# Windowed attention scores on Trainium2: penalty matmuls moved from the end to the front of a PSUM bank

## The chip, the cores and the metric

The kernel runs on one core of one Trainium2 chip. The metric is the device time of one execution in microseconds; the kernel before took 3160.31 us (median of three runs, 3152.64 to 3162.91).

## The reference, cut to what matters

Four layers are applied to an input of shape (4, 256, 48, 48), each as `x = x + layer(group_norm(x))`: an attention over 49 dilated taps, a convolution with binary weights, one with ternary weights, and layer 3, a linear attention over windows. Only layer 3 is touched:

```python
q = sigmoid(einsum('bchw,oc->bohw', x, Wq)); k = sigmoid(einsum('bchw,oc->bohw', x, Wk))
v = einsum('bchw,oc->bohw', x, Wv); v = v / max(norm(v, axis=channel_of_head), 1e-12)
for w in (1, 2, 4):                      # windows of 48, 24 and 12 rows and columns
    ws = H // w
    wk, wkv = box_sum(k, ws), box_sum(outer(k, v), ws)
    attn = einsum('bdhw,bdfhw->bfhw', q, wkv) / (einsum('bdhw,bdhw->bhw', q, wk) + 1e-6)
    outs.append(attn)
o = concatenate(outs, axis=1)
out = einsum('bchw,oc->bohw', o, Wout) + bout
```

There are 8 heads of 32 channels. A query at (row, column) sees the keys within half a window of it in both directions: 24, 12 or 6 rows and columns. Sigmoids are positive, so every score q.k is positive.

## The kernel before, in words

Layers 0 to 2 fill the time up to about 1416 us of the profiled execution, with the first projections of layer 3 among them. From there layer 3 computes numerators as masked scores times values.

**Tiling.** A block is one batch (4), one half of the channels with four heads (2) and one band of 8 rows (6): 48 blocks, in that order. Keys come in tiles of 8 rows by 16 columns, which makes 128 keys on the partitions, three tiles (`c` = 0, 1, 2) in a band. Queries are the moving operand, ordered by column and then by row: one column of the image is 8 elements.

**Steps.** `steps_of(rb)` (L1984) cuts a block into steps. A step holds the scores of four heads in two PSUM tiles `s` of two banks each, one bank of 512 fp32 for each head; the first tile is the pair of heads 0 and 1, the second that of heads 2 and 3. The pool `ps_s` has just these two tiles, so each step writes the banks that the step before it left. There are these kinds, counted over one batch and channel half (six bands):

- 32 *near* steps (`add_half`, L1968), for key bands within one band of the queries. A half has two products, each with its key tile: 320 columns of the moving operand for one and 192 for the other, which fill the bank.
- 12 *far* steps (`add_far`, L1954), for key bands three away: 280 and 168 columns, or 320 and 192.
- 8 *packed* steps with strips (`add_strips`, L1946) for key bands two away: three products of 128 columns for the widest window's strips, and one of 117 or 112 columns for the middle window.
- 6 packed steps that hold only products of the middle window (156 and 108, 84 and 81, or all four).

**Penalties.** The widest window is seen wholly by part of each tile; these keys are summed beforehand and added as a window state (`whole`, L2136). The rest, called the *strip*, needs a mask. The mask is added in PSUM: a bf16 matmul of `picks` (24 rows: 8 key rows and 16 key columns) with a row of costs adds -1024 where a key is not seen, and a ReLU in the evacuation makes these scores zero. `penalties()` (L165) lists the costs: for near steps the strip of each half (192 columns), for packed steps all four strips (384 columns), for far steps the whole tile (448 or 512). `PENALTY_AT` holds where each begins in the constant tile `masks`, which is loaded once, in bf16 (L1629).

**The order on TensorE.** `scores` (L2028) issues first the products, in the order product, pair, head, and then the penalties for each pair and head. The first product has `start=True`, the last penalty closes the bank. Four heads use four groups of 32 rows of the array. In the trace each fp32 product leaves two weight loads and two matmuls per head, a bf16 penalty one of each.

**Around it.** The loop over `stream` at the end of layer 3 issues for each step `n`: its scores, their evacuation (`masked`, L2055), and then the value products `acc` of step `n - 2` (`sums`, L2161). The evacuation is VectorE's mask multiplication for the middle window (`middle`) and a ReLU for the widest window (`widest`, on ScalarE, in far steps also on VectorE); the mask for the smallest window runs on GpSimd from SBUF. `acc` uses 128 rows by 32 columns of the array, `s` 32 rows by 128 columns. After each step `advance` lets background jobs (projections, key sums, norms, output products) issue a piece, within a budget that comes from `mask_time` and `sums_time`; these read `lo`, `hi` and `parts` of a step, not its products. Every engine runs its instructions in the order of the program (`InOrder`, L257), so the operations of a helper all carry L265 in the profile.

Of the kernel before, what the change touches and what calls it, by code (L numbers as in the profile page):

```python
# [23 lines left out]
B, C, H, W = 4, 256, 48, 48  # L24
# [3 lines left out]
RB = 8  # L28
# [66 lines left out]
def cols_seen(wi, c):  # L95
    h = HALVES[wi]
    return max(0, c * KC - h + (wi > 0)), min(W, c * KC + KC + h)


def cols_whole(c):  # L100

    return max(0, c * KC + KC - HALVES[0]), min(W, c * KC + HALVES[0])


def whole_ranges():
# [13 lines left out]
MID = W // 2  # L119
PARTS = [  # L120
    [(0, *cols_seen(0, 0)), (1, 0, MID)],
    [(1, MID, W), (2, *cols_seen(0, 2))],
]


def parts_seen(wi, half):

    got = []
    for c, x0, x1 in PARTS[half]:
        p0, p1 = cols_seen(wi, c)  # L130
        got.append((c, max(x0, p0), min(x1, p1)))
    return got


def strips(half):

    got = []
    for c, x0, x1 in PARTS[half]:
        f0, f1 = cols_whole(c)
        got.append((c, x0, f0) if x0 < f0 else (c, f1, x1))  # L140
    return got


def strip_columns(half):

    (_, x0, x1), (_, y0, _) = PARTS[half]
    (_, p0, p1), (_, q0, q1) = strips(half)
    assert p1 == x1 and q0 == y0
    return (p0 - x0) * RB, (x1 - x0 + q1 - q0) * RB
# [6 lines left out]
STRIPS = {}  # L156
# [7 lines left out]

def penalties():  # L165

    got = []
    for half in range(2):
        got.append(((0, half), strips(half), None))
    every = [(c, *part) for c, parts in STRIPS.items() for part in parts]  # L170
    got.append(((0, "strips"), every, None))
    for da, rows in FAR_ROWS.items():
        for half in range(2):
            got.append(((da, half), PARTS[half], rows))
    return got


def penalty_size(parts, rows):
    r0, r1 = rows or (0, RB)
    return sum(x1 - x0 for _, x0, x1 in parts) * (r1 - r0)  # L180


PENALTY_AT, _at = {}, 0
for _key, _parts, _rows in penalties():
    PENALTY_AT[_key] = _at, penalty_size(_parts, _rows)
    _at += PENALTY_AT[_key][1]
NPENALTY = _at
MASK_AT = [0, 0, MROWS[1] * MCOLS[1]]
PICK_AT = MASK_AT[2] + MROWS[2] * MCOLS[2]
PEN_AT = PICK_AT + P  # L190
NMASK = PEN_AT + NPENALTY
SM_ROOM = max(
# [5 lines left out]
def window_masks():  # L198
# [5 lines left out]
    for h, nr, m0, ncol in list(zip(HALVES, MROWS, MCOL0, MCOLS))[1:]:  # L204
# [4 lines left out]
        ms.append((rows[:, None, :] & cols[:, :, None]).reshape(P, -1))  # L209
    picks, costs = np.zeros((D, P)), np.zeros((D, NPENALTY))  # L210
    picks[ki, np.arange(P)] = 1
# [57 lines left out]
def conv_preact_kernel(  # L269
# [344 lines left out]
    with (  # L614
# [159 lines left out]
        def prepare_layer2():  # L774
# [34 lines left out]

            sums = smx.tile([P, NCT, 2, 2], F32, tag="sums", name="sums", bufs=1)  # L810
            pool.memset(sums, 0.0)
            yield
            ps = ps_cv.tile([P, 512], F32, tag="cv3", name="sum_ps")[:, 0 : 2 * NCT]
# [280 lines left out]
        def load_row(pool_, tag, a):  # L1094

            t = pool_.tile([P, NCT, K0, P], F32, tag=tag, name="wrow")
            sync.dma_start(
                out=t, in_=w1[:, a * K0 : (a + 1) * K0, :].rearrange("(ct p) k o -> p ct k o", p=P)
            )
            return t  # L1100
# [442 lines left out]
        with tc.tile_pool(name="wst", bufs=1) as wst:  # L1543
            for ct in range(NCT):
                fetch_x(0, ct)
            rows = [load_row(k1p, "k1", 0), load_row(vp, "v", MT), load_row(vp, "v", MT - 1)]
# [43 lines left out]
        with (  # L1590
# [11 lines left out]
            first = ExitStack()  # L1602
# [18 lines left out]
            for b in range(B):  # L1621
                if b + 1 < B:
                    filler = conv0(b + 1, {})
                else:
# [3 lines left out]
                    masks = wts3.tile([P, NMASK], BF16, name="masks")  # L1628
# [15 lines left out]
    with (  # L1644
# [14 lines left out]
        mask = {  # L1659
            i: masks[:, MASK_AT[i] : MASK_AT[i] + MROWS[i] * MCOLS[i]].rearrange(  # L1660
                "p (c r) -> p c r", c=MCOLS[i]
# [9 lines left out]
        for h in range(HEADS):  # L1671
            g = h % HG * D
# [245 lines left out]
        def rows_seen(wi, a, rb):  # L1918

            h = HALVES[wi]  # L1920
            return (
                max(0, a * RB - h + 1 - rb * RB),
                min(RB, a * RB + RB + h - rb * RB),
            )
# [5 lines left out]
        class Step:  # L1930
# [15 lines left out]
            def add_strips(self, a):  # L1946
                begin = self.columns
                for c, ranges in STRIPS.items():
                    at = self.add(a, c, ranges, (0, RB))
                    self.parts[0].append((a, c, ranges, (0, RB), at, self.columns - at))  # L1950
                self.penalties.append((begin, self.columns, PENALTY_AT[0, "strips"][0]))
                self.lo, self.hi = begin, self.columns

            def add_far(self, a, half):  # L1954
# [13 lines left out]
            def add_half(self, a, half):  # L1968

                da = a - self.rb  # L1970
                left = {}
                for c, x0, x1 in PARTS[half]:
                    left[c] = self.add(a, c, [(x0, x1)], (0, RB)) - x0 * RB
                self.lo, self.hi = strip_columns(half)
                self.penalties.append((self.lo, self.hi, PENALTY_AT[0, half][0]))
                for c, p0, p1 in strips(half):
                    self.parts[0].append((a, c, [(p0, p1)], (0, RB), left[c] + p0 * RB, (p1 - p0) * RB))
                for wi in range(1, NW):
                    rows = rows_seen(wi, a, self.rb)
                    for c, p0, p1 in parts_seen(wi, half):  # L1980
                        n = (p1 - p0) * (rows[1] - rows[0])
                        self.parts[wi].append((a, c, [(p0, p1)], rows, left[c] + p0 * RB, n))
# [35 lines left out]
        class Block:  # L2018
# [8 lines left out]

            def scores(self, st):  # L2028
                ss = [ps_s.tile([P, 2, 512], F32, tag="s", name="s") for _ in range(NPR)]
                for a, c, ranges, (r0, r1), at, n in st.products:  # L2030
                    for pr, s in enumerate(ss):
                        for j in range(2):
                            head = slice((2 * pr + j) * D, (2 * pr + j + 1) * D)
                            pe.matmul(
                                s[:, j, at : at + n],
                                kvs[self.b, self.ct, a][0][head, c, :],
                                of_columns(self.qs[head], ranges, r0, r1),
                                start=(at == 0),
                                stop=not st.penalties and at + n == st.columns,
                            )  # L2040
                for lo, hi, first in st.penalties:
                    for pr, s in enumerate(ss):
                        for j in range(2):
                            g = 2 * pr + j
                            rows = slice(g * D, g * D + RB + KC)
                            pe.matmul(
                                s[:, j, lo:hi],
                                picks[rows, :],
                                masks[rows, PEN_AT + first : PEN_AT + first + hi - lo],
                                start=False,  # L2050
                                stop=True,
                            )
                return ss

            def masked(self, st, ss):  # L2055

# [104 lines left out]
            def sums(self, wi, st, sms):  # L2161

                todo, acc = self.todo[wi], self.accs[wi]
                rows_ = acc.rearrange("p (w r) -> p w r", w=W)
                for k, (a, c, ranges, (r0, r1), _, _) in enumerate(st.parts[wi]):
                    for ranges_, o, n in self.alike(wi, ranges, r1 - r0):
                        for j in range(HG):
                            pe.matmul(
                                of_columns(rows_[D * j : D * (j + 1)], ranges_, r0, r1),
                                kvs[self.b, self.ct, a][1][:, c, j, :],  # L2170
                                sms[wi, k][:, j, o : o + n],
                                start=not self.reached[wi],
                                stop=(st is todo[-1] and k == len(st.parts[wi]) - 1),
                            )
                        for x0, x1 in ranges_:
                            self.reached[wi].update(range(x0, x1))
                if st is todo[-1]:
                    if self.i in inverses:
                        dve.tensor_mul(self.stage[:, wi, :], acc, inverses[self.i][:, wi, :])
                        divided.add((self.i, wi))  # L2180
                    else:
                        act.copy(self.stage[:, wi, :], acc)

        def of_columns(t, ranges, r0, r1):

# [110 lines left out]
        left = [groups[g] for g in made_first.left]  # L2296
# [88 lines left out]
        for n in range(len(stream) + LAG):  # L2385
            if n < len(stream):
                i, st, at, last = stream[n]
                if at == 0:
                    begun(i)
                ss = blocks[i].scores(st)  # L2390
# [3 lines left out]
            if n >= LAG:  # L2394
                i, st, at, last = stream[n - LAG]
# [64 lines left out]
```

## Time and profile before

| | us |
|---|---|
| median of three runs | 3160.31 |
| profiled execution | 3175.78 |
| its span, first to last instruction | 3174.0 |
| TensorE matmuls busy | 2852.3 |
| from 1416 us on: span / TensorE / GpSimd / VectorE / ScalarE busy | 1758 / 1661.2 / 1192.1 / 1074.4 / 712.3 |
| score products `s<-qs,ks`, 8704 records | 593.5 |
| penalties `s<-masks`, 1664 records | 169.2 |
| value products `acc<-sm,vs`, 18432 records | 606.6 |

PE stands for TensorE's matmuls, PEld for its weight loads, DVE for VectorE, ACT for ScalarE, POOL for GpSimd, SP for SyncE. A row of the groups names the tiles written and read, the shape and the count, then the busy time and the mean of one in ns, then the idle time of the engine before them and what ended it. In a shape such as 32*128 the first number is the rows and the second the columns of the array that are in use. Matmuls overlap, so the mean of one is longer than the distance from start to start; where a duration of streaming is wanted, the distance of starts is used. "issue" is time in which an engine waited for nothing that the profile shows.

### The profile page before, as it was taken

To read this page: it belongs to the slowest core of one execution; us is meant where nothing else is said; L and a number is where in the kernel's file an instruction comes from. 1 tells how busy PE (TensorE), PEld (TensorE's weight loads), DVE (VectorE), ACT (ScalarE), POOL (GpSimd) and SP (SyncE) were. 2 spreads that over 40 slices of the span, in tenths; PEclk is the share of its full clock that TensorE was granted. 3 is DMA by queue.
4 is the path that set the end of the run, shared out by engine and by line. 5 is a ranking of instruction groups with operands and counts; after the bars stand their busy time and mean duration, and the time that the engine had idled before them with its cause. 6 is when DMAs were issued, how large, how long until landed. Compare 5 with 4: busy or idle time off the path is not lost.

```text
span 3174.0 us, 99454 instructions
## 1 busy us (share of the span) xinstructions
PE 2852.3 (90%) x43082; PEld 2034.6 (64%) x43082; DVE 1989.3 (63%) x3779; ACT 991.4 (31%) x1959; POOL 1368.6 (43%) x1963
## 2 busy tenths in 40 slices
PE   3678999899989987889998899998999999999999
PEld 2556868677767866576665456665656666567665
DVE  7976658747864842276777565776546775555454
ACT  0002211121011134326643235552336533333322
POOL 0000012002000313046788876787856787744443
PEclk9889799999999998889999899999999999999999
DMA  8756412441333145324555665655644455611322
GB/s 277 214 161 188 154 68 103 127 127 49 132 114 113 57 124 158 113 80 138 160 181 174 184 203 157 183 174 161 169 127 145 142 173 156 166 41 43 97 73 66
DMA packets 380040, 434.10 MB, mean 137 GB/s; under 512 B 129843, under 2 KB 335443, under 8 KB 378451
## 3 DMA queue, kind: packets, MB, share of 16 engines
q1 hardware_dynamic: 378403, 425.76, 43.4%
q8 instruction: 341, 5.59, 0.7%
q0 software_dynamic: 144, 1.17, 0.2%
q10 hardware_dynamic: 1056, 0.79, 0.1%
q14 instruction: 96, 0.79, 0.1%
HBM read 288.11 MB, written 140.68 MB: 135 GB/s over the span
## 4 chain that ended last, share of the span: by engine, by line
PE 63%; DVE 11%; ACT 3%; POOL 3%; DMA 3%; issue 3%; SPq 1%; ACTq 0%; DVEq 0%; POOLq 0%
PE s L265 17%; PE cv L265 15%; PE acc L265 15%; PE out_ps L265 6%; PE proj_ps L265 5%; PE ap L265 3%; DVE sm L265 2%; DVE l2v L265 2%; ACT sm L265 1%; DVE v L265 1%; POOL sm L265 1%; PE keys_ps L265 1%; SPq L265 1%; DVE x L265 1%; DVE k L265 1%
## 5 line engine op out<-in xcount | busy, mean ns | idle before, releaser
L265 DVE TENSOR_TENSOR sm<-s,masks 128x448 f32<-128x448 f32 (+9 forms) x1408 | 620.1, 496 | 451.2 <-PE s L265 392.4
L265 POOL TENSOR_TENSOR sm<-sm,masks 128x704 f32<-128x704 f32 (+11 forms) x512 | 596.5, 1186 | 495.8 <-DVE sm L265 495.2
L265 ACT ACTIVATE sm<-s 128x384 f32<-128x384 f32 (+2 forms) x736 | 440.8, 608 | 734.2 <-PE s L265 583.9
L265 PE MATMUL cv<-vx,wt 128*128 128x288 f32 x2080 | 566.7, 429 | 90.5 <-DVE vx L265 49.2
L265 PE MATMUL s<-qs,ks 32*128 32x320 f32 (+10 forms) x8704 | 593.5, 361 | 36.7 <-ACT sm L265 26.3
L265 PE MATMUL acc<-sm,vs 128*32 128x128 f32 (+19 forms) x18432 | 606.6, 276 | 2.5 <-issue 2.1
L265 PEld LDWEIGHTS s<-qs,ks 32*128 32x128 f32 x8704 | 397.8, 186 | 264.1 <-issue 124.3
L265 PEld LDWEIGHTS acc<-sm,vs 128*32 128x32 f32 x18432 | 443.1, 110 | 176.5 <-issue 124.5
L265 PEld LDWEIGHTS cv<-vx,wt 128*128 128x128 f32 x2080 | 406.9, 200 | 213.6 <-issue 53.3
L265 POOL MEMSET v<- 128x16 f32 (+1 forms) x120 | 18.6, 214 | 765.2 <-DVE vx L265 639.0
L265 PE MATMUL cv<-v,wl 128*128 128x384 f32 x1152 | 227.2, 358 | 25.8 <-DVE x L265 8.2
L265 PEld LDWEIGHTS cv<-v,wl 128*128 128x128 f32 x1152 | 217.1, 198 | 37.0 <-issue 16.9
L265 DVE TENSOR_SCALAR sm<-s 128x896 f32<-128x896 f32 (+1 forms) x96 | 110.8, 1154 | 112.0 <-PE s L265 93.6
L265 PE MATMUL s<-masks 24*128 24x192 bf16 (+3 forms) x1664 | 169.2, 284 | 0.8 <-issue 0.8
L265 POOL TENSOR_TENSOR v<-l2v,v 128x384 fp32r<-128x384 f32 x96 | 108.4, 1158 | 119.5 <-ACT v L265 110.7
L265 PE MATMUL cv<-pad,wl 128*128 128x384 bf16 x864 | 145.6, 331 | 5.1 <-ACT pad L265 5.1
L265 POOL TENSOR_TENSOR nhi<-nhi,nq 128x384 f32<-128x384 f32 x144 | 147.3, 1044 | 0.0
L265 PE MATMUL out_ps<-o,wout_sb 128*32 128x384 f32 x1152 | 121.3, 490 | 7.2 <-ACT ns L265 3.7
L265 PEld LDWEIGHTS <-wl 128*128 128x128 bf16 x864 | 84.5, 98 | 65.6 <-issue 8.1
L265 PE MATMUL out_ps<-stage,wout_sb 128*32 128x384 f32 x1152 | 121.3, 487 | 0.0
L265 PE MATMUL ap<-seen,xT 120*128 120x120 f32 (+3 forms) x832 | 120.8, 306 | 0.0
L265 DVE TENSOR_TENSOR pt<-cs 128x184 f32<-128x184 f32 x144 | 120.4, 840 | 0.1
(176 smaller groups left out, 3398.6 us busy)
## 6 DMA issues: line engine op xcount, KB each, us to landing
wt<-wt SPq DMA_DIRECT2D x48, 768.0 KB
kb_d<-pt SPq DMA_DIRECT2D x48, 576.0 KB
rc<-r_d SPq DMA_DIRECT2D x192, 144.0 KB
nhi<-kb_d SPq DMA_DIRECT2D x120, 192.0 KB
nlo<-kb_d SPq DMA_DIRECT2D x88, 192.0 KB
o_d<-stage SPq DMA_DIRECT2D x24, 576.0 KB
o<-o_d SPq DMA_DIRECT2D x24, 576.0 KB
wl<-wl_d SPq DMA_DIRECT2D x16, 768.0 KB
```

What stands on the lines that cost most here:

```text
L265: return lambda *args, **kwargs: self.tc.keep_in_program_order(op(*args, **kwargs))
```

## The change

- The costs of near steps are no longer the strips alone. `whole_parts(half)` takes the strip of one tile and the whole columns of the other, which lie side by side in the bank: 320 columns for each half. The two halves form one table of 640 columns. The strips' table of the packed steps is dropped: `of_penalties` reads the four strips as two runs of 192 columns out of the near table. `NPENALTY` goes from 2688 to 2560.
- `scores` issues the penalties first. They carry `start=True`; products then have `start=False` wherever a step has penalties, and the last product closes the bank. Steps without penalties keep their order.
- No product may lie across the edge of the penalties, so `add_half` cuts at the strip: the 320 columns become 192 and 128. A near step has three products (192, 128, 192) in place of two.
- `lo`, `hi`, `parts` and so the evacuation, the value products and the budgets of the background jobs stay.

```diff
+def whole_parts(half):
+    first, second = PARTS[half]
+    return [strips(half)[0], second] if half == 0 else [first, strips(half)[1]]
...
 def penalties():
-    got = []
-    for half in range(2):
-        got.append(((0, half), strips(half), None))
-    every = [(c, *part) for c, parts in STRIPS.items() for part in parts]
-    got.append(((0, "strips"), every, None))
+    (c0, x0, _), (c1, y0, y1) = whole_parts(0)
+    (d1, z0, z1), (d2, _, w1) = whole_parts(1)
+    assert c1 == d1 and y1 == z0 == MID
+    got = [((0, "near"), [whole_parts(0)[0], (c1, y0, z1), whole_parts(1)[1]], None)]
...
+for _half in range(2):
+    _n = penalty_size(whole_parts(_half), None)
+    PENALTY_AT[0, _half] = PENALTY_AT[0, "near"][0] + _half * _n, _n
+_every = [(c, *part) for c, parts in STRIPS.items() for part in parts]
+NSTRIP = penalty_size(_every, None) // 2
+STRIPS_APART = PENALTY_AT[0, "near"][1] - NSTRIP
...
-                self.penalties.append((begin, self.columns, PENALTY_AT[0, "strips"][0]))
+                self.penalties.append((begin, self.columns, None))
...
                 for c, x0, x1 in PARTS[half]:
-                    left[c] = self.add(a, c, [(x0, x1)], (0, RB)) - x0 * RB
+                    left[c] = self.columns - x0 * RB
+                    cuts = {x0, x1}
+                    for d, *ends in whole_parts(half):
+                        if d == c:
+                            cuts.update(ends)
+                    cuts = sorted(cuts)
+                    for y0, y1 in zip(cuts, cuts[1:]):
+                        self.add(a, c, [(y0, y1)], (0, RB))
                 self.lo, self.hi = strip_columns(half)
-                self.penalties.append((self.lo, self.hi, PENALTY_AT[0, half][0]))
+                (c, x0, _), (d, _, x1) = whole_parts(half)
+                self.penalties.append((left[c] + x0 * RB, left[d] + x1 * RB, PENALTY_AT[0, half][0]))
...
             def scores(self, st):
                 ss = [ps_s.tile([P, 2, 512], F32, tag="s", name="s") for _ in range(NPR)]
-                for a, c, ranges, (r0, r1), at, n in st.products:
+                self.penalise(st, ss)
+                for m, (a, c, ranges, (r0, r1), at, n) in enumerate(st.products):
...
-                                start=(at == 0),
-                                stop=not st.penalties and at + n == st.columns,
+                                start=m == 0 and not st.penalties,
+                                stop=m == len(st.products) - 1,
                             )
+                return ss
+
+            def penalise(self, st, ss):
...
                             pe.matmul(
                                 s[:, j, lo:hi],
                                 picks[rows, :],
-                                masks[rows, PEN_AT + first : PEN_AT + first + hi - lo],
-                                start=False,
-                                stop=True,
+                                of_penalties(rows, first, hi - lo),
+                                start=True,
+                                stop=False,
                             )
-                return ss
...
+        def of_penalties(rows, first, n):
+            if first is not None:
+                return masks[rows, PEN_AT + first : PEN_AT + first + n]
+            at = PEN_AT + PENALTY_AT[0, "near"][0]
+            both = masks[rows, at : at + 2 * STRIPS_APART].rearrange("p (g n) -> p g n", g=2)
+            return both[:, :, 0:NSTRIP]
```

More of the change, by code (lines that the diff above doesn't have):

```diff
@@ L187 @@
 NPENALTY = _at
+for _half in range(2):
[4 more added lines that the diff above has]
+STRIPS_APART = PENALTY_AT[0, "near"][1] - NSTRIP
+assert penalty_size(_every[:2], None) == NSTRIP and _every[:2] == [strips(0)[0], strips(0)[1]]
+assert _every[2:] == strips(1) and strips(0)[1][1] == 0 and strips(1)[0][2] == W
+assert PENALTY_AT[0, "near"][0] + 2 * STRIPS_APART <= NPENALTY
 MASK_AT = [0, 0, MROWS[1] * MCOLS[1]]
@@ L2037, in scores @@
                                 of_columns(self.qs[head], ranges, r0, r1),
-                                start=(at == 0),
-                                stop=not st.penalties and at + n == st.columns,
-                            )
+                                start=m == 0 and not st.penalties,
+                                stop=m == len(st.products) - 1,
+                            )
+                return ss
+            def penalise(self, st, ss):
                 for lo, hi, first in st.penalties:
+                    assert all(at + n <= lo or at >= hi or (lo <= at and at + n <= hi) for *_, at, n in st.products)
                     for pr, s in enumerate(ss):
```

## The prediction, made before the changed kernel ran

> **What bounds the kernel now.** I read the page first: engines, slices, the chain that ended last.
>
> ```profile
> span 3174.0 us, 99454 instructions
> PE 2852.3 (90%) x43082; PEld 2034.6 (64%) x43082; DVE 1989.3 (63%) x3779; ACT 991.4 (31%) x1959; POOL 1368.6 (43%) x1963
> PE   3678999899989987889998899998999999999999
> PE 63%; DVE 11%; ACT 3%; POOL 3%; DMA 3%; issue 3%; SPq 1%; ACTq 0%; DVEq 0%; POOLq 0%
> PE s L265 17%; PE cv L265 15%; PE acc L265 15%; PE out_ps L265 6%; PE proj_ps L265 5%; PE ap L265 3%; DVE sm L265 2%; DVE l2v L265 2%; ACT sm L265 1%; DVE v L265 1%; POOL sm L265 1%; PE keys_ps L265 1%; SPq L265 1%; DVE x L265 1%; DVE k L265 1%
> ```
>
> TensorE ends most of the chain, and the scores `s`, which the change edits, are its largest line. They start at 1416.6 us. The busy times from there to the end, and who waited for what there:
>
> ```profile
> core 0: us, PE busy (x) PEld busy (x) DVE busy (x) ACT busy (x) POOL busy (x), PEclk, DMA share, GB/s
> 1416.00:3174.00 1758.00, 1661.17 (x37250) 1089.78 (x37250) 1074.38 (x2011) 712.25 (x1435) 1192.05 (x1558) 0.98 0.47 142
> ...
> PE s L265 <- ACT sm L265: 26.3, 49, 4.0
> ...
> DVE sm L265 <- PE s L265: 486.1, 370, 6.9
> ...
> ACT sm L265 <- PE s L265: 583.9, 331, 9.5
> ```
>
> TensorE is busy 1661 of 1758 us; VectorE and ScalarE wait for its scores, far more than it waits for them. Now one near step in the timeline, asked in small windows so that each start is seen:
>
> ```profile
> 2510.19 0.55 PE L265 MATMUL s<-qs,ks 32*128 32x320 f32 x4
> 2510.56 0.61 PE L265 MATMUL s<-qs,ks 32*128 32x320 f32 x8
> 2510.83 0.50 PE L265 MATMUL s<-qs,ks 32*128 32x192 f32 x8
> 2511.16 0.26 PE L265 MATMUL s<-masks 24*128 24x192 bf16 x4
> 2511.35 0.34 PE L265 MATMUL acc<-sm,vs 128*32 128x160 f32 x4
> ```
>
> The four heads' matmuls start together. An fp32 product leaves two records per head. From first to second is 0.37 us, from second to the next product 0.27, though both stream 320 columns. Over all steps that begin undisturbed I find medians of 373 and 269 ns: **104 ns of every opening are not streaming**. The weight loads tell why:
>
> ```profile
> L265 PEld LDWEIGHTS s<-qs,ks x8704: 180/185/333, 1416.6 to 3153.5; 32*128 32x128 f32 x198
> ...
> L265 PEld LDWEIGHTS <-masks x1664: 90/93/162, 1417.4 to 3153.7; 24*128 24x128 bf16 x185
> L265 PEld LDWEIGHTS acc<-sm,vs 128*32 128x32 f32 x18432 | 443.1, 110 | 176.5 <-issue 124.5 <-POOL sm L265 0.6 <-ACT sq L265 0.5
> ```
>
> A 128-column fp32 load is recorded at 181 ns when it opens a step, the bf16 load of the picks at 93, a 32-column fp32 load at 107. After `acc` opens, its first interval is 26 ns over streaming (161 for 160 columns, which need 135). So 181 recorded goes with 104 exposed, 107 with 26: exposed time is the record less about 80.
>
> [...] the trace has a further 112 ns between the end of streaming in `s` and `acc` (192 from a 192-column penalty, 325 from a 512-column one, 0.416 ns per column).
>
> **The change, part by part.** There are 58 steps in each of 8 blocks of batch and channel half: 32 near, 12 far, 8 packed with a penalty, 6 without one, whose code path stays. Per step, in ns on TensorE:
>
> *The opening.* The bf16 load replaces the fp32 one as the exposed load. I take 12 (93 less 80); the bounds are 0 (the load's wait is now only on TensorE itself, so it can precede the release of the bank) [...]. The fp32 load of the first product must then fit under the penalty's streaming: at least 320 columns x 0.416 = 133, against 104. That a bf16 matmul can cover the next fp32 load is seen in layer 2, in full-array mode; the fp32 matmul starts at the bf16 pace (162 ns; 4 cases of 4):
>
> ```profile
> 446.63 0.49 PE L265 MATMUL cv<-pad,wl 128*128 128x384 bf16 x2
> 446.96 0.41 PE L265 MATMUL cv<-vx,wt 128*128 128x288 f32 x1
> ```
>
> Two records start 0.16 us apart in the first line, the fp32 one after the same 0.16. No run here shows it in 32-row mode. Saving: 104 - 12 = 92 in each of 416 steps.
>
> *Near steps, penalty.* 320 columns in place of 192: 128 x 0.416 = +53.
>
> *Near steps, split.* The 320-column product becomes 192 and 128: four more fp32 products, so 8 more matmul records and as many loads. A record of 192 columns takes 162, one of 128 columns 111.5 in packed steps (the weight load is its floor, products of 84 columns take 112 too). Two records: 2 x (162 + 111.5 - 269) = +9; I use 10.
>
> *The end.* An fp32 product is now last. After the last fp32 record of a step without penalties `acc` starts 219 later, at 81 and at 108 columns alike[...]. After a penalty it is 112 over streaming too. Nothing for near and far; packed steps end on a load-bound product that now hides nothing, about +8. VectorE and ScalarE get their signal from the last matmul as before.
>
> *Near:* -92 + 53 + 10 = -29, taken as -28. *Far:* -92. *Packed:* -84. So a near step should go from 1160 (its undisturbed median from first matmul to the following `acc`) to 1132, far ones from 1160 and 1293 to 1068 and 1201, packed ones from 1255 to 1171. Sum: 256 x 28 + 96 x 92 + 64 x 84 = 7.2 + 8.8 + 5.4 = 21.4 us.
>
> *Waits and queues.* The waits for the banks' readers move to the penalties. Behind the wait of the second pair of heads stand now all products of the first pair; before, the first product of the first pair ran during that wait. 210 of 462 openings are staggered so. It costs nothing: in staggered near steps `acc` comes 1177 after the second pair's released load (far 1177 and 1311), 17 over the undisturbed step, so the late pair runs its whole step after its release, whatever the first has done; in the new order too. If the early work did help, it would be worth at most one record, 269 ns x 210 = 56 us, but these 1177 exclude it. A penalty issues no DMA; compiled, ScalarE's, VectorE's and SP's streams are the same line by line, and POOL's differs in one load of masks, 4460 columns for 4588: nothing.
>
> *How much reaches the end.* The undisturbed durations times counts give 534 us for all steps; "PE s" holds 30.7% of the chain over these 1758 us, 540 us. So practically every step lies on the chain, and where TensorE waits for a bank the shorter step shortens that loop as well. TensorE is idle 97 us in 1758 (6%); I take nine tenths: 19.3 us. The profiled execution (3175.8 us, its span 3174.0 and 1.8 around it) would become 3156.5; it lies 15.5 over the median, from which I forecast 3160.3 - 19.3 = 3141.0.
>
> **Rivals.** (A) *Slower: the first product's load isn't hidden behind the bf16 penalty.* Against it: the free bf16-to-fp32 change above. For it: that was another array mode, and no step here has both types on the same row group in this order. Then a near step pays 53 + 10 + 12 = +75, a far one +12, a packed one +20: 19.2 + 1.2 + 1.3 = 21.7, nine tenths 19.5: 3180. With x ns exposed per opening the balance is 416 x (104 - x) = 256 x 63 + 64 x 8, x = 64: above 64 ns the kernel gets slower. (B) *The bf16 load saves half*: x = 53, 21.2 - 16.6 = 4.6, nine tenths 4.1: 3156, no change. The record of 93 speaks against it. (C) *The gain goes into waits*: in the chain VectorE, ScalarE and POOL at `sm` hold 9% and DMAs some more; a pair of scores ready earlier may wait for an evacuation still in its queue. With only half kept, 10 us: 3150.5. Against it: 486 and 584 us of their waiting for `s`. That the change does something else is excluded by the compiled streams.
>
> **Numbers.** Forecast 0.68, C 0.11, B 0.09, A 0.12. The forecast's own range is 3134 (nothing exposed, 26.6 us, all kept) to 3148. With the scatter of the runs (3152.6 to 3162.9) and the cases B and C it is 3130 to 3158; A and the tails stay out. A measurement of this kernel can tell about 0.3%, 9.5 us, from no change. Faster by more: 0.67 + half of C = 0.73; within: 0.15; slower: 0.12.
>
> **What would show it.** Right: penalties as the first `s` matmuls after `acc`, the next fp32 record 133 to 160 ns after a near penalty, undisturbed near steps near 1132 and far 448 ones near 1068, products of 128 columns at 112 a record, "PE s" of the chain some 20 us less. Wrong: about 240 ns from penalty to first product (A); near steps over 1160; or short steps and longer waits of TensorE for ScalarE and VectorE (C).

## The result, and the profile after

The changed kernel takes 3143.45 us (median of seven runs, 3134.32 to 3150.29), the one before, run beside it, 3160.88 (seven, 3152.64 to 3172.99). The ratio is 0.9938 with a 95% interval of 0.992 to 0.9955: 19.6 us less, between 14 and 25. The forecast was 19.3 less.

The page of the changed kernel, the rows that answer to those shown of before: span, busy times, and the chain that ended last, by engine and by line.

```profile
span 3141.7 us, 103006 instructions
PE 2792.0 (89%) x45130; PEld 2024.0 (64%) x45130; DVE 1985.7 (63%) x3779; ACT 991.6 (32%) x1959; POOL 1372.3 (44%) x1963
PE 59%; DVE 14%; POOL 4%; DMA 4%; ACT 3%; issue 3%; SPq 1%; ACTq 0%; DVEq 0%; POOLq 0%
PE cv L281 15%; PE s L281 15%; PE acc L281 13%; PE out_ps L281 5%; PE proj_ps L281 5%; DVE sm L281 4%; PE ap L281 2%; DVE l2v L281 2%; SPq L281 1%; POOL sm L281 1%; POOL nhi L281 1%; DVE v L281 1%; ACT sm L281 1%; PE keys_ps L281 1%; DVE x L281 1%
```

"PE s" has fallen from 17% to 15% of the chain and "DVE sm" has risen from 2% to 4%. In microseconds of layer 3 the chain has 479 of "PE s" for 539 before, and 139 of "DVE sm" for 77. TensorE has 2048 matmuls and 2048 weight loads more than before and is busy 60 us less. Part of that is no merit of the edit. The two profiled spans differ by 32.3 us, but 17.5 of these lie before the first score matmul, which comes at 1399.1 us here and at 1416.6 before, in a stretch that the edit doesn't touch; over all profiles of this study that moment falls anywhere from 1397.6 to 1416.6, with the edit or without. So I compare layer 3 alone, from the first score matmul to the end of the last step: 1737.7 us before, 1722.9 after, 14.8 less.

The same near step as in the prediction, from the timeline of the changed kernel, asked in small windows (start in us, duration, engine, line, instruction, count):

```profile
2489.37 0.31 PE L281 MATMUL s<-masks 24*128 24x320 bf16 x4
2489.52 0.33 PE L281 MATMUL s<-qs,ks 32*128 32x192 f32 x4
2489.68 0.55 PE L281 MATMUL s<-qs,ks 32*128 32x192 f32 x12
2489.85 0.55 PE L281 MATMUL s<-qs,ks 32*128 32x128 f32 x12
2489.95 0.61 PE L281 MATMUL s<-qs,ks 32*128 32x128 f32 x12
2490.23 0.33 PE L281 MATMUL s<-qs,ks 32*128 32x192 f32 x4
2490.49 0.34 PE L281 MATMUL acc<-sm,vs 128*32 128x160 f32 x4
```

The penalties now come first, and the first fp32 record follows 0.15 us later; from first matmul to `acc` it is 1.12 us, where before it was 1.16. Medians over all undisturbed steps, in ns:

| from first `s` matmul to `acc` | before | forecast | after | change |
|---|---|---|---|---|
| near | 1160 | 1132 | 1120 | -40 |
| far, 448 columns | 1160 | 1068 | 1056 | -104 |
| far, 512 columns | 1293 | 1201 | 1190 | -103 |
| packed with penalty | 1255 | 1171 | 1151 | -103 |
| packed without | 617, 681, 1106 | the same | the same | 0 |

Times their counts: 256 x 40 + 96 x 104 + 64 x 103 = 10.2 + 10.0 + 6.6 = **26.8 us** of shorter steps. Layer 3 gave 14.8 of them.

Two rows of the groups show the opener's price, the penalties and their weight loads (busy us, mean ns, then idle time before them and what ended it):

```profile
L281 PE MATMUL s<-masks 24*128 24x320 bf16 (+3 forms) x1664 | 188.6, 326 | 45.2 <-ACT sm L281 32.6
L281 PEld LDWEIGHTS <-masks 24*128 24x128 bf16 x1664 | 66.1, 91 | 241.4 <-issue 171.9
```

The penalty group now carries the idle time, 45.2 us, where before the change 36.7 us stood ahead of the products: the waits for the bank have moved to it, as forecast. The load is recorded at a mean of 91, where it was 95 before.

### The profile page after: what moved, and what is told of

The parts are those of the page before. It is cut to its first block, busy times and chain, and to the rows that moved or that the text cites. A ratio compares the mean times of both kernels' runs of the same rounds, so it can differ in the third digit from the quotient of the medians.

```text
span 3141.7 us, 103006 instructions
## 1 busy us (share of the span) xinstructions
PE 2792.0 (89%) x45130; PEld 2024.0 (64%) x45130; DVE 1985.7 (63%) x3779; ACT 991.6 (32%) x1959; POOL 1372.3 (44%) x1963
## 3 DMA queue, kind: packets, MB, share of 16 engines
q10 hardware_dynamic: 1056, 0.79, 0.1%
## 4 chain that ended last, share of the span: by engine, by line
PE 59%; DVE 14%; POOL 4%; DMA 4%; ACT 3%; issue 3%; SPq 1%; ACTq 0%; DVEq 0%; POOLq 0%
PE cv L281 15%; PE s L281 15%; PE acc L281 13%; PE out_ps L281 5%; PE proj_ps L281 5%; DVE sm L281 4%; PE ap L281 2%; DVE l2v L281 2%; SPq L281 1%; POOL sm L281 1%; POOL nhi L281 1%; DVE v L281 1%; ACT sm L281 1%; PE keys_ps L281 1%; DVE x L281 1%
## 5 line engine op out<-in xcount | busy, mean ns | idle before, releaser
L281 PE MATMUL cv<-vx,wt 128*128 128x288 f32 x2080 | 558.0, 424 | 90.2 <-DVE vx L281 51.1
L281 PE MATMUL s<-qs,ks 32*128 32x192 f32 (+9 forms) x10752 | 510.9, 310 | 1.3 <-issue 0.4
L281 PEld LDWEIGHTS s<-qs,ks 32*128 32x128 f32 x10752 | 410.6, 187 | 27.6 <-issue 17.6
L281 PE MATMUL cv<-v,wl 128*128 128x384 f32 x1152 | 226.4, 357 | 26.8 <-DVE x L281 9.2
L281 PEld LDWEIGHTS cv<-v,wl 128*128 128x128 f32 x1152 | 216.5, 197 | 37.8 <-issue 17.7
L281 PE MATMUL s<-masks 24*128 24x320 bf16 (+3 forms) x1664 | 188.6, 326 | 45.2 <-ACT sm L281 32.6
L281 PEld LDWEIGHTS <-masks 24*128 24x128 bf16 x1664 | 66.1, 91 | 241.4 <-issue 171.9
```

What stands on the lines that cost most here:

```text
L281: return lambda *args, **kwargs: self.tc.keep_in_program_order(op(*args, **kwargs))
```

## The experiments

Layer-3 numbers below are of the one profiled execution of each kernel; medians and ratios are of the timed runs, and a "gain" is one less the ratio, times the partner's time.

**1. One part of the change at a time.** The kernel before, with the penalty first in far and packed steps only:

```diff
+ahead_ = bool(st.penalties) and not bool(st.parts[2])
+if ahead_:
+    self.penalise(st, ss, True)
...
-    start=(at == 0),
-    stop=not st.penalties and at + n == st.columns,
+    start=m == 0 and not ahead_,
+    stop=m == len(st.products) - 1 and (ahead_ or not st.penalties),
```

> Far and packed steps open with their penalty as in the changed kernel, near steps stay as before (192-column penalty last, two products). Theory (the bf16 opener hides the fp32 weight load, step by step): undisturbed near steps stay at 1160 ns, far ones fall to 1056 and 1189, packed ones to 1151, 16.6 us of steps in all; of that 0.65 to 1 arrives at the end, 11 to 17 us less than before (ratio 0.9965 to 0.995). Rival (the gain was one of waits between the pairs of heads, spread over all steps): a gain in proportion to the steps changed, 160 of 416, about 7 us (0.998). Rival (the gain lies outside layer 3): layer 3 as long as before.

Measured: 3141.09 us, ratio 0.9929 (0.9905 to 0.9952): 22 us faster, 15 to 30, so the rival of 7 us falls. Far steps 1056 and 1189, packed 1151, near 1160 as before. Layer 3 is 13.1 shorter of 16.6 us of shorter steps. A far step of this kernel in the timeline:

```profile
2379.61 0.37 PE L265 MATMUL s<-masks 24*128 24x448 bf16 x4
2379.80 0.93 PE L265 MATMUL s<-qs,ks 32*128 32x168 f32 x16
2380.66 0.44 PE L265 MATMUL acc<-sm,vs 128*32 128x280 f32 x4
```

The 448-column penalty streams 187 ns and the product starts 0.19 later; `acc` comes 1.05 after the penalty. As far as the runs can tell, this part alone brings as much as the whole change.

The other part: the changed kernel, with the penalty first in near steps only (wide, with the split), and last in far and packed ones:

```diff
-self.penalise(st, ss)
+ahead_ = bool(st.penalties) and bool(st.parts[2])
+if ahead_:
+    self.penalise(st, ss, True)
...
+if not ahead_:
+    self.penalise(st, ss, False)
```

> Near steps as in the changed kernel (320-column penalty first, products 192, 128, 192), far and packed steps with the penalty last as before. Theory: undisturbed near steps at 1120 ns, far ones at 1160 and 1293, packed at 1255; 256 x 40 ns = 10.2 us of steps, 6 to 10 us less than before (0.998 to 0.997). Rival (waits between the pairs, in proportion to the steps): about 11 us (0.9965). Rival (the near edit costs what it saves): no change, near steps at 1160.

Measured: 3163.13 us, ratio 0.9991 (0.9979 to 1.0004): 2.8 us faster, between 6.6 faster and 1.3 slower. Its near steps are at 1120, 40 ns shorter, 10.2 us in all; far and packed ones are as before. But layer 3 of the profile is 3.5 us *longer* than before. So the steps of the near edit are shorter, and the kernel isn't.

Only what the near edit adds, nothing of what it saves: wide penalty and split, penalties last in every step:

```diff
-ahead_ = bool(st.penalties) and bool(st.parts[2])
+ahead_ = bool(st.penalties) and False
```

> The near steps' wide penalty and split products alone: every penalty stays last as before, but near steps have 320 penalty columns in place of 192 and three products in place of two. Theory: 53 ns of penalty columns and 9 ns of split per near step, so 1222 ns undisturbed, 15.9 us of steps in all, 10 to 16 us slower than before (1.003 to 1.005). Rival (the split costs more, for its 8 additional weight loads a step): near steps over 1240 ns and over 20 us.

Measured: 3179.95 us, ratio 1.0053 (1.0036 to 1.007): 16.8 us slower. Near steps take 1224 ns, so the two terms of the prediction, 53 and 10, are 64. This *cost* arrives in full (layer 3 +14.4).

**2. The changed kernel once more, for its trace.** No edit.

> The changed kernel once more, for a second profile beside the first. If the 26.8 us that its undisturbed steps are shorter are lost in part to a lasting cause, the same blocks of layer 3 lose again: the first profile gained 2 to 7 us in six of eight blocks of batch and channel half, but lost 5.0 in the fourth, and the new one will too, and the half-clock windows stand at the same places. If it was chance, the fourth block gains some 3 us this time and layer 3 is 1730 to 1738 us long, in place of 1742.

Measured: 3149.75 us, ratio 0.9943 (0.9924 to 0.9962); layer 3 at 1720.8, 16.9 less than before. Layer 3 has eight blocks of batch and channel half. If the gain were even, each would give 3.35 us. The first profile after has -2.9, -1.1, -3.1, **+5.0**, -2.0, +0.4, -3.8, -7.2, the second -2.3, -0.1, -4.0, **+8.7**, -3.2, -4.7, -4.2, -7.1. The fourth block lost time twice. But both are set against one and the same profile of before, the two profiles of the changed kernel differ by 3.6 us in this block and by 5.1 in the sixth, and the far and packed edit alone, with near steps as before, lost 2.4 there too. So a lasting loss in this block isn't shown. In it TensorE pauses at the same two places in both profiles, for 2.05 and 3.1 us, then 2.2 and 4.1, with nothing waited for. The first of them in the timeline of the changed kernel, and SP's queue at that time:

```profile
2229.86 0.29 PE L281 MATMUL kv_ps<-vs,keys 128*32 128x32 f32 x10
2232.19 0.33 PE L281 MATMUL kv_ps<-vs,keys 128*32 128x32 f32 x14 [2.05 <-issue]
```

```profile
2227.67 5.27 SPq L281 DMA_DIRECT2D rc<-r_d  x4
```

Ten of 24 like matmuls run, then TensorE stands still, then the other 14 run: no operand, semaphore or bank separates them. The stretches around it (busy time and count of each engine, granted clock, busy share of the DMA engines, GB/s):

```profile
core 0: us, PE busy (x) PEld busy (x) DVE busy (x) ACT busy (x) POOL busy (x), PEclk, DMA share, GB/s
2227.00:2230.00 3.00, 3.00 (x98) 2.36 (x86) 2.47 (x7) 1.34 (x3) 3.00 (x4) 1.00 0.95 317
2230.00:2232.00 2.00, 0.14 (x14) 0.03 (x1) 0.51 (x2) 0.12 (x1) 2.00 (x3) 1.00 1.05 241
2232.00:2240.00 8.00, 7.81 (x162) 5.20 (x166) 2.56 (x5) 2.06 (x4) 5.70 (x7) 0.79 0.24 68
```

The DMA engines are full (0.95 and 1.05 of their time), four broadcast loads of `rc` (the inverse norms) having just been issued; TensorE is without work for 2 us; then its granted clock is 0.79 over 8 us, for it is halved during 3.4 of them. The pages also list a DMA queue of the kind "instruction". Its rows before and after (packets, MB, share of the engines' time):

```profile
q8 instruction: 341, 5.59, 0.7%
```

```profile
q8 instruction: 354, 5.80, 0.8%
```

The split brings 4096 records more, and 13 packets more (0.21 MB / 13 = 16 KB each). From this came a theory: the near edit pays for its shorter steps in instructions, which are late when the DMA engines are full.

One half of this the traces settle. In the pause shown, a packet of this queue moves from 2229.34 to 2230.59 us, and TensorE goes on 1.60 us after its end. Over all 14 profiles, from the first score matmul to the last step, TensorE pauses 98 times for more than 0.6 us with nothing waited for. Every one of these pauses ends 1.1 to 1.7 us (median 1.4) after the end of such a packet, though packets come only every 9 us or so; of the matmuls that did not wait, 10 to 12% start at that distance. So these pauses are waits for instructions. What makes a packet late is not settled so: in the kernel before, the DMA engines were over half busy during eight of the nine pauses, and idle during the ninth. Here are TensorE's pauses with nothing waited for, in layer 3, before and after (total us, times, longest):

```profile
PE kv_ps L265 <- issue: 7.0, 4, 2.5
PE s L265 <- issue: 2.9, 4, 1.3
PE acc L265 <- issue: 2.1, 3, 1.0
PE out_ps L265 <- issue: 1.6, 2, 0.8
```

```profile
PE kv_ps L281 <- issue: 8.9, 5, 3.1
PE acc L281 <- issue: 4.0, 8, 1.0
PE out_ps L281 <- issue: 2.4, 3, 1.2
```

With the rows not shown it is 13.6 us before and 18.2 after, and 15.3 in the second profile of the changed kernel.

**3. Is it the full DMA engines?** The 192 broadcast loads of inverse norms are left out, here from the kernel before; the division by the norms is thereby left out of the computation (a tile of ones is used).

```diff
-rc = op.tile([P, NW, NB], F32, tag="rc", name="rc")
-for g in range(HG):
-    sync.dma_start(
-        out=rc[g * D : (g + 1) * D].rearrange("p w n -> p (w n)"),
-        in_=r_d[b][rb, t * HG + g]
-        .rearrange("w n -> (w n)")
-        .partition_broadcast(D),
-    )
-rcs.append(rc)
+rcs.append(rc_ones)
```

> The kernel before without the loads of the inverse norms (192 DMAs of 144 KB that copy one line to 32 partitions each): the numerators are multiplied by a constant tile of ones, so the division is left out. It is the base for the next three. Theory on where the near steps' gain went (TensorE starves for instructions while these copies fill the DMA engines, and each pause also costs a half-clock window): pauses of TensorE without a semaphore fall from 11.5 us to under 5, half-clock time in layer 3 from 65 us to under 50, and the time by 10 to 25 us. Rival (pauses come from semaphores of other engines): pauses stay, the time changes by under 5 us.

The same edit on the changed kernel, on the near part alone, and on the far and packed part alone:

> The changed kernel, with the loads of the inverse norms left out in the same way (no division). Theory (starved instructions ate part of the gain): against the base without these loads nearly all of the 26.8 us of shorter steps arrives, 22 to 27 us less. Rival (the near steps' gain goes into waits for ScalarE, VectorE and GpSimd): 15 to 19 us less, as with the loads.

> Near steps alone as in the changed kernel, the loads of the inverse norms left out (no division). Theory (starved instructions): 8 to 10 us less than the base without these loads, where with the loads it was 3. Rival (waits for other engines): 0 to 4 us less again.

> Far and packed steps alone opened by their penalty, the loads of the inverse norms left out (no division). Both theories: 14 to 17 us less than the base without these loads, close to its 16.6 us of shorter steps; together with the near steps alone it adds up to the changed kernel without these loads.

Measured: before without the loads 3149.07 us, ratio to before 0.9943 (0.9931 to 0.9955), 18 us faster; its pauses fall from 13.6 to 5.5 us:

```profile
PE kv_ps L265 <- issue: 3.1, 3, 1.3
PE out_ps L265 <- issue: 1.2, 2, 0.8
PE acc L265 <- issue: 0.9, 2, 0.6
PE s L265 <- issue: 0.3, 1, 0.3
```

The other three kernels too pause less without the loads (by 4 to 10 us), so the loads make pauses: that much is shown. Pauses under 5 us and half-clock time under 50 were forecast; 5.5 and 52 came. The DMA engines need not be full during a pause: in two of the four over 0.6 us here they are 4 and 6% busy (41 and 91% in the 3 us ahead of it). Against this new base (differences of the means, with two standard errors) the whole change brings 18.9 +- 7.4 us, the near part alone 5.3 +- 5.6, far and packed alone 15.2 +- 7.1 (14 to 17 was forecast). If these loads had eaten the near part's gain, it would have come back here to its 10.2. By the runs this is not excluded, for the interval reaches 10.9; in the one profile layer 3 gained 1.6. So the theory that the near gain is lost to these loads has a profile against it, and the runs decide neither for it nor for its rival.

**4. Or GpSimd?** The second block takes longest (243 us before, where the first takes 215), and GpSimd's work on norms falls into it. The subtractions and multiplications of the norms are left out, so that the norms are wrong:

```diff
-pool.tensor_sub(hi[:, wi, n:RB], hi[:, wi, n:RB], lo[:, wi, n:RB])
...
-flat = hi[:, wi].rearrange("p r w -> p (r w)")
-pool.tensor_mul(flat, flat, qf)
```

> The kernel before with GpSimd's subtractions and multiplications for the norms left out (the loaded sums go into the norm product as they are); loads, order and all else stay. It is the base for the next two. Theory (in the blocks of the first three batches' second channel half something other than TensorE's stream sets the pace, and GpSimd's norm work is it): these three blocks become several us shorter, the time 10 us or more. Rival (it is the evacuation of the scores by VectorE and ScalarE): the time changes by under 5 us.

> The changed kernel with the same GpSimd work left out. Theory (GpSimd's norm work holds three of eight blocks): those three blocks now gain some 3 us each as the other five do, and 22 to 27 us of the 26.8 arrive against the base without that work. Rival (evacuation by VectorE and ScalarE): 15 to 19 us as with that work, and the three blocks gain nothing.

> Near steps alone as in the changed kernel, the same GpSimd work left out. Theory (GpSimd's norm work): 8 to 10 us less than the base without that work. Rival (evacuation): 0 to 5 us less, as with that work.

Measured: before without it 3137.75 us, ratio 0.9916 (0.9885 to 0.9947), 27 us faster, its second block at 228.8, the fourth 7.9 shorter and the sixth as before. Against this base the whole change brings 11.5 +- 9.5 us by means, and layer 3 is 22.0 shorter, the most of the four pairs with the whole change: blocks -3.2, -2.7, -3.3, +0.2, -3.2, -2.3, -4.6, -3.0. The second and sixth block now give their share. But the near part alone, for which 8 to 10 us less was forecast, is 6.3 +- 6.4 us slower by means and 1.7 by medians, layer 3 +7.2. For the near part this theory falls.

**5. A version of its own.** Far and packed penalties first everywhere; the near edit in the blocks that had gained only (first halves, and the last batch), in the others the near step as before:

```diff
+two = {wide: [steps_of(rb, wide) for rb in range(NRB)] for wide in (True, False)}
+steps = {(b, ct): two[ct == 0 or b == B - 1] for b in range(B) for ct in range(NCT)}
```

> Far and packed steps open with their penalty everywhere; near steps do so, with wide penalty and split, only in the five blocks of batch and channel half in which the profiles show the gain arriving (first channel halves, and the last batch), and stay as before in the other three. If the near edit only costs in those three blocks (more instructions to fetch, more waits), this is 2 to 5 us faster than the changed kernel (ratio to before 0.9925). If the blocks' difference was chance: as the changed kernel or up to 4 us slower (0.994 to 0.995).

Measured: 3141.85 us, ratio 0.9935 (0.9911 to 0.9958). Its layer 3 is 1708.1 in the profile, 14.8 less than the changed kernel's, but by its runs it can't be told from the changed kernel (7.1 +- 6.5 faster than the repeat, on another chip) nor from far and packed alone (2.4 +- 7.4). No version here clearly beats the changed kernel. Its profile is a warning all the same: layer 3 is 29.5 us shorter than before, more than the 23.0 of its shorter steps, and TensorE pauses 5.0 us *less* than before, with 2560 more records. What one profile shows beside the steps thus moves by several us and more.

The pairs side by side, in us, as change against the partner (minus is shorter). "Steps" is what the undisturbed steps save. Layer 3 is divided into "scores" (the 464 steps from first score matmul to the next other one, with TensorE's idle time just ahead of them) and "all else". "Pauses" and "half clock" are TensorE's time with nothing waited for and at half its clock, from the first score matmul to the end of the span:

| edit, and base of both | steps | scores | all else | layer 3 | runs | pauses | half clock |
|---|---|---|---|---|---|---|---|
| whole, before | -26.8 | -33.9 | +19.1 | -14.8 | -19.6 (-25 to -14) | +4.6 | +16.1 |
| whole again, before | -26.8 | -34.9 | +18.1 | -16.9 | -18.0 (-24 to -12) | +1.7 | +20.7 |
| whole, both without `rc` loads | -26.8 | -29.2 | +18.1 | -11.1 | -18.9 +- 7.4 | +5.9 | +24.0 |
| whole, both without norm work | -26.8 | -35.2 | +13.2 | -22.0 | -11.5 +- 9.5 | +6.3 | +1.6 |
| far and packed, before | -16.6 | -22.7 | +9.6 | -13.1 | -22 (-30 to -15) | -0.4 | +17.7 |
| far and packed, without `rc` loads | -16.6 | -19.0 | +2.7 | -16.3 | -15.2 +- 7.1 | -0.3 | +7.8 |
| near, before | -10.2 | -6.3 | +9.8 | +3.5 | -2.8 (-6.6 to +1.3) | +4.5 | +13.6 |
| near, without `rc` loads | -10.2 | -8.2 | +6.7 | -1.6 | -5.3 +- 5.6 | +2.1 | +5.8 |
| near, without norm work | -10.2 | -13.6 | +20.7 | +7.2 | +6.3 +- 6.4 | +9.1 | +3.7 |
| wide and split, last | about +16 | +7.7 | +6.7 | +14.4 | +16.8 (+11 to +22) | +3.8 | +1.9 |
| far and packed, near in five blocks, before | -23.0 | -26.5 | -3.0 | -29.5 | -20.6 (-28 to -13) | -5.0 | +5.3 |

## Why the prediction was right, and where it was not

**The opening: right.** Intervals from penalty to first fp32 record are 146 ns at 320 columns (133 of streaming), 175 at 384 (160), 200 at 448 (187), 226 at 512 (213): 13 to 15 exposed, where 12 was forecast from the recorded loads. In the record the bf16 load that opens a step is half as long as the fp32 load that opened it before (91 ns for 181), but far less than half of the 104 exposed shows. Rival A (240 ns from penalty to first product) and rival B (53 exposed, about half of the 104) fall: these 13 to 15 ns are all that shows of both loads, so the fp32 load hides behind the bf16 penalty in 32-row mode too.

**Penalty and split: right.** 53 + 10 was forecast, 1224 - 1160 = 64 measured where nothing else changes.

**The end: mis-sized.** "Nothing for near and far" and "packed steps ... about +8" rested on 112 ns over streaming ahead of `acc`. With an fp32 product last it is 101: from the last 192-column record to `acc` 261, not 272. Both count from the first of the four heads; from the last of the four it is 91 and 93, and the four start within 10 ns now, within 20 before. That is most of the 12 ns by which the near, far and packed steps undercut the forecast, 20 in the packed ones, where the 8 didn't come either. So the steps gave 26.8 us and not 21.4.

**Staggered openings: right.** They are about as frequent as before (196 of 462, 210 before), and staggered far and packed steps shortened likewise. All steps together, staggered ones among them, take 38.3 us less (621.2 to 582.9), and TensorE's idle time just ahead of them rises by 4.4 (29.6 to 34.1). That is 33.9 together, more than the 26.8 of the undisturbed steps.

**"I take nine tenths": the step that failed.** It was applied to all kinds of step alike, and fits neither part. Far and packed steps were to give 0.9 x 14.2 = 12.8 us and gave 22 (15 to 30) and 15.2 +- 7.1, where their steps are 16.6 shorter: all of it. The near edit was to give 6.5 and gave 2.8, 5.3 and -6.3 in three pairs, each with an interval near +-6 or less; weighted by these they average 1.7 +- 2.9, but they differ from each other by more than these intervals allow, so the average is known about half as well as that. The near steps did become shorter, by 10.2 us, and most of this didn't reach the end. **The total came out right by luck, because two misses cancel**: longer savings in the steps (26.8 for 21.4) and a smaller share of them kept (14.8 and 16.9 of 26.8 in the two profiles).

The nine tenths were taken from TensorE's idle share, 6%, with no term for idle time that grows. In layer 3 its busy time fell by 37.6 us, but its idle time rose by 22.8 (90.9 to 113.7; to 110.1 in the second profile). Rival C, the gain going into waits, was right in part: at `s` the waits for ScalarE and VectorE grew by 9.6 us (28.5 to 38.1), and "PE s" lost 60 us of the chain where 20 was forecast, while "DVE sm" gained 62. But the scores with the waits ahead of them still gave more than was forecast. What is missing lies in the rest of layer 3, which took 19.1 us longer: 13.7 of idle time ahead of other work (7.0 of it with nothing waited for, 4.8 of projections waiting for ScalarE), and 5.3 of other matmuls that took longer.

**What the sum left out** is an item for 4096 more records on TensorE. The seven pairs with the near edit everywhere, the repeat among them, and the split alone all pause more with nothing waited for (+1.7 to +9.1 us); the two pairs without the split don't (-0.4, -0.3). That the pauses are waits for instructions is shown above (98 of 98 end 1.1 to 1.7 us after a packet of that queue). That more instructions make more of them is likely and not shown: the kernel with the near edit in five blocks pauses less than the one before, the two profiles of the changed kernel are 2.9 us apart, and no kernel added instructions and nothing else. And pauses are not the whole loss: the split alone has them too (+3.8) and loses no more than its longer steps.

Time at half clock grew in every kernel with a penalty first, by 1.6 to 24.0 us. In the half-clock windows matmuls start about twice as far apart (products of 384 columns into `out_ps`: 640 to 642 ns, 323 outside them, in the two traces of before and after), so at most half of this time is lost. An estimate of pauses plus half of the added half-clock time comes near what is missing of the steps for the change (4.6 + 8.1 = 12.7 us, 12.0 missing) and its repeat (12.0, 9.9 missing), but not in the parts (8.5 where 3.5 are missing in far and packed, 10.9 where 17.4 are in near without norm work). So it gives the size of the loss, not its place. That the pauses bring the half clock about is only argued, from their order in time in one place. Against it, no half-clock window follows the pause of 2.63 us that begins at 1631.2 us of the changed kernel, and in the far and packed pair on the kernel before, half-clock time grew by 17.7 us without more pauses.

**Open.** How the near edit's loss divides between pauses, half clock and waits, for its three pairs differ; what makes an instruction packet late; what fills the 91 to 93 ns over streaming ahead of `acc`, for the runs show its length and not its cause; and whether near steps would pay with the 192-column penalty first and no split. That wasn't tried: a product would lie across the edge of the penalty, which the changed kernel excludes by an assertion; no run here shows what such a product does.

## What to carry to other kernels

A short bf16 matmul that has to run anyway made a good opener for a PSUM bank here: its 128-column weight load showed for 13 to 15 ns where the fp32 load showed for 104, and it hid the fp32 load behind its own streaming of 133 to 213 ns. Take that where it is free; where it must be bought with wider or more instructions, the shorter step of the timeline isn't yet a gain (10.2 us of near steps, some 2 us at the end), so run that part by itself. Where a total agrees with its forecast, compare the parts all the same: here the agreement hid two errors. And where an engine stands still with nothing waited for, look at the instruction queue: here all 98 pauses over 0.6 us ended 1.1 to 1.7 us after a packet of it.

## What the runs showed of the hardware that was not expected

- TensorE can stand still for up to 4.1 us amid like matmuls with nothing waited for, and goes on 1.1 to 1.7 us after the end of a 16 KB instruction packet (98 of 98 pauses over 0.6 us, in 14 profiles). Leaving out 192 broadcast loads took these pauses from 13.6 to 5.5 us and the kernel from 3167.15 to 3149.07.
- TensorE falls to half clock for short windows (3.4 to 13.7 us in the first profile after), 10 of 12 of them at the same places of the program (within 4 us) in both profiles of the changed kernel: 79 and 84 us in all from the first score matmul on, and 63 in the kernel before, though TensorE is busy 93% of layer 3.
- Counted from the last of the four heads' matmuls, the gap ahead of `acc` over streaming is much the same after an fp32 product (91 ns) and after a bf16 penalty (93); four bf16 penalties start within 20 ns of each other, the fp32 records that now end a step within 10.
